# Linear attention on one core: the keys' products with values issued every fourth step instead of every second

## The chip, the cores and the metric

The kernel runs on one core of one Trainium2 chip. The metric is the device time of one execution in microseconds (us). Before the change three runs took 2346.34, 2346.76 and 2348.77 us, a median of 2346.76 us. Engines are named as the profile names them: PE is TensorE (matmuls), PEld its loads of weights, DVE is VectorE, ACT is ScalarE, POOL is GpSimd, SP is SyncE, from whose queue most DMAs are issued.

## What is computed

A decoder layer on x of 2 sequences x 2048 tokens x 512, in float32: linear attention, cross attention to 154 context tokens, and a mixture of eight experts with two shared units. The change touches the linear attention alone (16 heads of 32, 128 features a head):

```python
qkv = x @ w_qkv                       # x is layernormed
q_proj = _elu1(jnp.einsum('bhnd,hdf->bhnf', q, proj_matrix))
k_proj = _elu1(jnp.einsum('bhnd,hdf->bhnf', k, proj_matrix))
kv = jnp.einsum('bhnf,bhnd->bhfd', k_proj, v)
attn = jnp.einsum('bhnf,bhfd->bhnd', q_proj, kv)
k_sum = k_proj.sum(axis=2)
z = 1.0 / (jnp.einsum('bhnf,bhf->bhn', q_proj, k_sum) + 1e-08)
out = (attn * z[..., None]).reshape(b, n, d) @ w_out + b_out
```

## The kernel before

**Tiling.** The 4096 tokens are 8 blocks of 512, four to a sequence. A block has four chunks of four heads (128 columns of the model), and a chunk has four tiles of 128 tokens. So the keys take 8 x 4 x 4 = 128 steps n, one for each (block, chunk, tile).

**The loop of the key steps (L1277 to L1304).** Step n does five things in program order:

1. `dense.fill` (L1279) issues some nine or ten matmuls from a list of projections waiting to be made: keys (`pk`), values (`pv`) and queries (`pq`), and near the end the context's keys and values (`xpk`, `xpv`). Each is a chain of 12 full 128x128 matmuls of 512 columns. `dense` also counts matmuls for things that are due later, such as reading a stored tile back (`dense.after`).
2. `key_features` (L393): four matmuls `pp` (L402) into a PSUM bank of the pool `sc` (four banks), then Relu and Exp on ACT (L364, L365) and a combination on DVE (L366) into `e_k`, 128x512, and an addition into `kacc` on POOL (L407). `e_k` is one of nine buffers of the tag `kp` (L102), which other tiles share.
3. (b, c, t) is appended to the list `todo` (L1297).
4. From n = 66 on, `query_step` (L1257) makes the features of one head of the queries of the sequence whose keys are done: one matmul `pqp` (L479), then the same ACT and DVE work into `e_q` (head 0, tag `kp`) or `eq` (heads 1 to 3, a pool of five buffers, L83).
5. On some steps, `sums_step` (L1265). It makes `key_values` (L410) for all of `todo` but the last two entries, the newest first, and, when the queries' step is the last head of a chunk (h == 3), the numerators (L485) and denominators (L507) of the chunk before.

**Column matmuls.** `key_values`, `numerators` and `denominators` use a stationary operand of 32 columns and write 32 partitions of PSUM, one head at a time: `pkv[h*32:(h+1)*32]`, `pn`, `pd`. The trace shows each of them as 128*32 and counts two instructions for each of the program's matmuls (1024 for the 512 of `pkv`). They go through a helper, all at line L230:

```python
def matmul(self, *args, **kw):
    ins = nc.tensor.matmul(*args, **kw)
    tc.keep_in_program_order(ins)
```

The rest of the order on each engine is set by the framework's scheduler, which also picks the buffer of each tile. A group of L230 matmuls with no other matmul between them is called a run here.

**The condition before** is `n % 2 and len(todo) > LAG` with LAG = 3: sums are made at every odd n from 3 on, two tiles' products at a time. On n with n % 4 == 1 (from 69 on) the numerators and denominators follow in the same call; on n with n % 4 == 3 the call has only the two tiles' products.

**After the 128 steps** six more (L1305) finish the sums of the second sequence; `summary` (L430) turns the products over for use by the queries. The queries of the second sequence follow with the attention's output projection (L1317 to L1356), then cross attention (L1360) and the experts (L1457).

Of the kernel before, what the change touches and what calls it, by code (L numbers as in the profile page):

```python
# [31 lines left out]
LAG = 3  # L32
# [5 lines left out]
def decoder_layer(  # L38
# [62 lines left out]
    def half(name, dtype=F32):  # L101
        return work.tile([P, 512], dtype, tag="kp", name=name, bufs=9)  # L102
# [8 lines left out]
    def load_row(d, name):  # L111
        row = rowp.tile([P, D], F32, tag="row", name=name)
        nc.sync.dma_start(out=row, in_=d.to_broadcast([P, D]))
        return row
# [11 lines left out]
    def split_weight(raw, name, busy=False):  # L126

        hi = eight([P, NC, D], FR, f"{name}_hi")
        lo = eight([P, NC, D], FR, f"{name}_lo")
        for k in range(NC):  # L130
            if isinstance(raw, list):
                part = raw[k]
            else:
                part = load_tile(raw, 0, k, name)
            if busy:
                nc.gpsimd.tensor_scalar(hi[:, k], part, 1.0, None, ALU.mult)
            else:
                nc.scalar.copy(hi[:, k], part)
            low(lo[:, k], part, hi[:, k], nc.gpsimd if busy or k % 2 else nc.vector)
        return hi, lo  # L140
# [94 lines left out]
    def fl(k, f):  # L235
        return int((k + 1) * f + 1e-6) - int(k * f + 1e-6)
# [156 lines left out]
    def key_features(b, c, t):  # L393
        if (b % bpb, c, t) == (0, 0, 0):
            bt = b // bpb
            kaccs.append(eight([P, H * FEAT], F32, f"kacc{bt}"))
            nc.gpsimd.memset(kaccs[bt], 0.0)
        rows = slice(t * P, (t + 1) * P)
        pp = sc.tile([P, 4, FEAT], F32, tag="sc", name=f"pp{b}_{c}_{t}")
        for h in range(4):  # L400
            head = slice((4 * c + h) * FEAT, (4 * c + h + 1) * FEAT)
            nc.tensor.matmul(  # L402
                pp[:, h], lhsT=stks[b, c][:, h, rows], rhs=pst[:, head], start=True, stop=True
            )
        kp = features(pp.rearrange("p h f -> p (h f)"), f"k{b}_{c}_{t}")
        acc = kaccs[b // bpb][:, c * 512 : (c + 1) * 512]
        nc.gpsimd.tensor_tensor(acc, acc, kp, ALU.add)  # L407
        kps[b, c, t] = kp
# [63 lines left out]
    def load_queries(b, c):  # L472
        qsts[b, c] = eight([3 * HD, 4, TB], FR, f"qst{b}_{c}")
        stack(qsts[b, c], qd[b][c])
# [69 lines left out]
    def load_numerators(b):  # L544
        nums[b] = eight([P, NC, TB], F32, f"num{b}")
        nc.gpsimd.dma_start(out=nums[b], in_=numd[b])

    def load_reciprocals(b, c):
        two = pair_of(f"zr{b}_{c}").bitcast(F32)
        for h in range(4):  # L550
            nc.sync.dma_start(
                out=two[h * HD : (h + 1) * HD],
                in_=zds[b][h : h + 1, c : c + 2].to_broadcast([HD, 2, TB]),
            )
        for i in range(2):
            zrs[b, c + i] = two[:, i]
# [41 lines left out]
    def context_load():  # L598
        craw = eight([P, NC, nkeys], F32, "craw")
        nc.sync.dma_start(out=craw, in_=chunked(ctx_t))  # L600
        for i in range(2):
            ct.append(eight([P, NC, nkeys], FR, f"ct{i}"))
        nc.scalar.copy(ct[0], craw)
        low(ct[1], craw, ct[0], nc.gpsimd)

    def context_key(c, w):
        pk = bank(f"xpk{c}")[:, :nkeys]
        yield from project(pk, w, c * P, ct)
        kf = half(f"kf{c}")[:, :nkeys]
        nc.vector.tensor_scalar(kf, pk, bk_sb[:, c : c + 1], scale, ALU.add, ALU.mult)  # L610
        hl = pair_of(f"xkhl{c}", nkeys)
        nc.scalar.copy(hl[:, 0], kf)
        low(hl[:, 1], kf, hl[:, 0])
        store_pair(ckd[c], hl)

    def context_value(bt, first, w, row):
        n = min(P, keys - first)
        at = bt * keys + first
        pv = bank(f"xpv{bt}_{first}")
        yield from product(  # L620
            pv[:n, :],
            [
                (
                    (ct[0][:, k, at : at + n], ct[1][:, k, at : at + n]),
                    (w[0][:, k, :], w[1][:, k, :]),
                )
                for k in range(NC)
            ],
        )
        v = half(f"v{bt}_{first}")  # L630
        nc.vector.tensor_tensor(v[:n], pv[:n, :], row[:n], ALU.add)
        nc.sync.dma_start(out=vd[bt][first : first + n], in_=v[:n])
# [619 lines left out]
    todo = []  # L1252
# [4 lines left out]
    def query_step(m):  # L1257

        at, h = divmod(m, 4)
        if at < bpb * NC:  # L1260
            if h == 0 and at + 1 < bpb * NC:
                load_queries(*chunks[at + 1])
            query_features(*chunks[at], h)

    def sums_step(m):  # L1265


        columns.batch()
        ready = len(todo) if m >= (nblk - bpb) * per - shift else len(todo) - LAG + 1
        for i in reversed(range(ready)):  # L1270
            key_values(*todo.pop(i))
        at, h = divmod(m, 4)
        if m >= 0 and at and h == 3:
            numerators(*chunks[at - 1])
            denominators(*chunks[at - 1])

    for n in range(nblk * per):  # L1277
        b, c, t = n // per, n // NT % NC, n % NT
        dense.fill(58 if n == 0 else fl(n, 9.25) if n < 32 else fl(n, 9.5))  # L1279
        if (b, c, t) == (nblk - 1, 0, 0):  # L1280
            context_load()
        if (b, c, t) == (nblk - 1, 1, 0):
            xwk = split_weight(wk_t, "xwk")
            dense.add(*(context_key(i, xwk) for i in range(NC)))
        if (b, c, t) == (nblk - 1, 2, 0):
            xwv = split_weight(wv_t, "xwv")
            bvr = half("bvr")
            nc.sync.dma_start(out=bvr, in_=bv.to_broadcast([P, D]))
            for bt in range(batches):
                dense.add(*(context_value(bt, at, xwv, bvr) for at in range(0, keys, P)))  # L1290
        if (b, c, t) == (nblk - 1, 3, 0):
            load_numerators(0)
            load_reciprocals(0, 0)
            bout = load_row(b_out, "bout")
        dense.until(stks, (b, c))
        key_features(b, c, t)
        todo.append((b, c, t))  # L1297
        m = n - bpb * per - shift
        if m == -4:
            load_queries(0, 0)  # L1300
        if m >= 0:
            query_step(m)
        if n % 2 and len(todo) > LAG:
            sums_step(m)  # L1304
    for m in range((nblk - bpb) * per - shift, (nblk - bpb) * per + NT):  # L1305
        dense.fill(5)
# [150 lines left out]
    for n, (group, u) in enumerate(todo3):  # L1457
# [18 lines left out]
        for s, part in enumerate(parts):  # L1476
# [19 lines left out]
            if ahead[0]:  # L1496
                (ln, tr), (ln2, tr2) = ahead
                todo = (ln, [], tr[:2], tr[2:] + ln2, [], tr2[:2], tr2[2:])
# [89 lines left out]
```

## Time and profile before

| what | value |
|---|---|
| median of the three runs | 2346.76 us |
| the profiled execution, its own time | 2340.21 us |
| its span, first to last instruction | 2338.5 us |
| mean granted clock of PE in it | 0.984 |
| PE busy in the span | 2241.0 us, 96% |
| DVE, POOL, ACT busy | 72%, 52%, 47% |
| L230 `pkv`, instructions | 1024, from 44.5 to 475.7 us |
| L230 `pn` and `pd`, instructions | 512, from 263.0 to 641.2 us |

How to read it: busy times are sums over one execution, and a matmul's duration overlaps that of the next, so the distance from start to start tells what a matmul costs and the duration doesn't. In a timeline, x16 means sixteen instructions merged into one row; the bracket at the end gives idle time of the engine before the row and what ended it. PEclk is the granted share of PE's full clock. A row of a windows view has the stretch, its length, then the busy time of each engine with its count of instructions, the granted clock, the share of the DMA engines' time and GB/s.

### The profile page before, as it was taken

The numbers are of one execution on the slowest core, as the hardware profiler recorded it, in microseconds if no ns is written. First come the engines' busy times: TensorE is split into PE (matmuls) and PEld (weight loads), VectorE is DVE, ScalarE is ACT, GpSimd is POOL, SyncE is SP. The second block draws the span as 40 slices with busy tenths as digits, with TensorE's granted clock in tenths as the row PEclk, the third lists the DMA queues.
The fourth block names the chain that finished last, engine by engine and source line by source line (L and its number), as shares of the span: only waits on it lengthen the run. The fifth ranks groups of instructions, "written<-read, shape, count | busy, mean of one in ns | idle before, by whom it ended". The sixth has DMA issues, their size and how long they took to land.

```text
span 2338.5 us, 35133 instructions
## 1 busy us (share of the span) xinstructions
PE 2241.0 (96%) x11978; PEld 1733.3 (74%) x11978; DVE 1680.3 (72%) x2777; ACT 1104.9 (47%) x2598; POOL 1223.2 (52%) x1086
## 2 busy tenths in 40 slices
PE   7999999899989999999999999999999999999999
PEld 5888777655577777766777777888778887788887
DVE  6554555668577776877877786777887778977777
ACT  4555776756566766775343333222333222432221
POOL 5545433547475554553655554544564455754543
PEclk9999999999999999999999999999999999999999
DMA  6555778899965665565665646555447556575553
GB/s 210 180 171 174 208 210 228 248 255 266 258 201 159 173 175 155 172 199 203 243 240 221 223 175 258 209 222 207 158 180 275 207 207 236 193 276 202 211 189 131
DMA packets 194896, 485.63 MB, mean 208 GB/s; under 512 B 26970, under 2 KB 46810, under 8 KB 174782
## 3 DMA queue, kind: packets, MB, share of 16 engines
q1 hardware_dynamic: 192990, 477.30, 61.5%
q0 software_dynamic: 1728, 6.09, 0.9%
q8 instruction: 95, 1.56, 0.3%
q14 instruction: 83, 0.68, 0.1%
HBM read 345.01 MB, written 138.31 MB: 207 GB/s over the span
## 4 chain that ended last, share of the span: by engine, by line
PE 48%; DVE 9%; DMA 5%; POOL 4%; issue 3%; ACT 2%; SPq 0%; ACTq 0%; DVEq 0%; POOLq 0%
PE pg L1053 25%; PE pf L1166 10%; PE po_x L148 3%; PE pf L148 2%; PE xpq L148 2%; PE pc L745 2%; PE xpt L725 1%; PE psc L693 1%; DMA rgu<-in_w_up 1%; DVE u L1073 1%; DVE xo L118 1%; POOL hp L118 1%; DVE wq L118 1%; DVE u L1085 1%; DMA xsx<-x 1%
## 5 line engine op out<-in xcount | busy, mean ns | idle before, releaser
L1053 PE MATMUL pg<-xo,wq 128*128 128x512 f32 x3360 | 825.7, 393 | 7.2 <-ACT s L1064 3.5
L1053 PEld LDWEIGHTS pg<-xo,wq 128*128 128x128 f32 x3360 | 630.2, 189 | 149.3 <-ACT s L1064 7.1
L1187 DVE TENSOR_TENSOR sum<-sum,pf 128x512 f32<-128x512 f32 x376 | 250.5, 682 | 61.1 <-PE pf L1166 53.5
L407 POOL TENSOR_TENSOR kacc<-kacc,e_k 128x512 f32<-128x512 f32 x128 | 165.9, 1297 | 225.6 <-DVE e_k L366 203.6
L703 ACT ACTIVATE xe<-psc,nb 128x154 f32<-128x154 f32 x512 | 194.4, 403 | 63.0 <-DVE nb L700 47.4
L708 POOL TENSOR_TENSOR xe<-xe,sm 128x616 f32<-128x616 f32 x128 | 156.7, 1232 | 108.1 <-DVE sm L707 73.7
L1116 POOL TENSOR_TENSOR u<-u,gr 128x512 f32<-128x512 f32 x48 | 63.8, 1328 | 255.7 <-DVE u L1085 244.3
L1166 PE MATMUL pf<-ht,wdo 128*128 128x512 f32 x696 | 187.4, 393 | 1.0 <-DVE sum L1187 1.0
L366 DVE SCALAR_TENSOR_TENSOR e_k<-pp,e_k 128x512 f32<-128x512 f32 x128 | 87.4, 685 | 107.9 <-ACT e_k L365 101.8
L1166 PE MATMUL pf<-hb,wdo 128*128 128x512 f32 x522 | 148.2, 399 | 6.0 <-DVE sum L1187 5.9
L1166 PEld LDWEIGHTS pf<-ht,wdo 128*128 128x128 f32 x696 | 129.8, 188 | 30.7 <-DVE sum L1187 1.7
L1084 ACT ACTIVATE u<-u 128x512 f32<-128x512 f32 x80 | 50.6, 633 | 211.1 <-DVE u L1073 208.5
L148 PE MATMUL pf<-wd,hp 128*128 128x512 f32 x528 | 134.0, 400 | 6.2 <-DVE hp L118 3.0
L700 DVE TENSOR_REDUCE nb<-psc 128x2 f32<-128x308 f32 x256 | 111.9, 467 | 31.1 <-PE psc L693 30.9
L148 PEld LDWEIGHTS pf<-wd,hp 128*128 128x128 f32 x528 | 99.7, 190 | 33.1 <-DVE hp L118 3.9
L1166 PEld LDWEIGHTS pf<-hb,wdo 128*128 128x128 f32 x522 | 97.4, 189 | 30.4 <-DVE sum L1187 7.7
L1073 DVE TENSOR_TENSOR u<-u,pg 128x512 f32<-128x512 f32 x160 | 107.7, 679 | 10.5 <-PE pg L1053 9.7
L703 ACT ACTIVATION_READ_ACCUMULATOR xe<-psc,nb 128x1 f32 x512 | 111.6, 218 | 0.0
L364 ACT ACTIVATE e_k<-pp 128x512 f32<-128x512 f32 x128 | 76.8, 601 | 69.9 <-PE pp L402 64.4
L693 PEld LDWEIGHTS psc<-xkst,xst 96*128 96x128 f32 x512 | 76.1, 193 | 35.2 <-ACT xe L703 18.9
L693 PE MATMUL psc<-xkst,xst 96*128 96x154 f32 x512 | 90.3, 284 | 12.3 <-ACT xe L703 8.4
L402 PEld LDWEIGHTS pp<-pst,kst 96*128 96x128 f32 x512 | 75.8, 191 | 26.8 <-issue 9.9
(280 smaller groups left out, 5143.2 us busy)
## 6 DMA issues: line engine op xcount, KB each, us to landing
wq<-wqs SPq DMA_DIRECT2D x90, 1024.0 KB
wqs<-wq SPq DMA_DIRECT2D x30, 1024.0 KB
wdo<-wds SPq DMA_DIRECT2D x29, 1024.0 KB
kst<-kd SPq DMA_DIRECT2D x96, 256.0 KB
qst<-qd SPq DMA_DIRECT2D x96, 256.0 KB
xst<-xqd SPq DMA_DIRECT2D x96, 256.0 KB
wdo<-wds SPq DMA_DIRECT2D x29, 768.0 KB
kd<-khl SPq DMA_DIRECT2D x32, 512.0 KB
```

The costliest lines, as they stand in the source:

```text
L148: nc.tensor.matmul(dst, lhsT=a, rhs=b, start=n == 0, stop=n == len(todo) - 1)
L364: nc.scalar.activation(e, src, AF.Relu, scale=-1.0)
L366: nc.vector.scalar_tensor_tensor(e, src, 0.0, e, ALU.max, ALU.add)
L407: nc.gpsimd.tensor_tensor(acc, acc, kp, ALU.add)
L693: nc.tensor.matmul(psc[:, i], lhsT=xsts[b, c][:, h, t * P : (t + 1) * P], rhs=ksts[bt, c][:, h, :], start=True, stop=True,)
L700: nc.vector.tensor_reduce(nb[:, two], psc, AX.X, ALU.max, negate=True)
L703: nc.scalar.activation(e[:, h, :], psc[:, i], AF.Exp, bias=nb[:, h : h + 1], accum_out=sm[:, h : h + 1],)
L708: nc.gpsimd.tensor_tensor(e, e, sm.unsqueeze(2).to_broadcast([P, 4, keys]), ALU.mult)
L1053: nc.tensor.matmul(pb, lhsT=w[:, p, i, k, :], rhs=xop[:, q, k, :], start=first and m == 0, stop=m == len(todo) - 1, skip_group_check=True,)
L1073: nc.vector.tensor_tensor(dst, dst, pb, ALU.add)
L1166: nc.tensor.matmul(banks[i], lhsT=w[:, p, i * P : (i + 1) * P], rhs=t[q], start=new and m == 0, stop=m == len(TERMS) - 1, skip_group_check ...
L1187: nc.vector.tensor_tensor(dst, dst, banks[i], ALU.add)
```

## The change

One condition in the loop of the key steps:

```diff
         if m >= 0:
             query_step(m)
-        if n % 2 and len(todo) > LAG:
+        if n % 4 == 1 and len(todo) > LAG:
             sums_step(m)
```

`sums_step` is now called at n = 5, 9, ... 125, and each call makes the products of four tiles instead of two. The queries' step is m = n - 66, so that n % 4 == 1 is h == 3: every call that makes numerators and denominators is still made, at the same step, with four tiles' products ahead of them in place of two. What is not called any more is `sums_step` at n = 3, 7, ... 127. At the time of a call `todo` holds six tiles in place of four, so six `e_k` buffers of the nine are held rather than four. The last entries, which the call at n = 127 took before, are taken by the first call after the loop (m = 63).

Every matmul, activation and DMA of the program is there as before, in the same number; the scheduler, which sees another list, also places others of them differently, on every engine.

## The prediction

> **What bounds the kernel now.** I read the page first, then the busy times by stretch, then who makes PE wait, and last the order of PE's instructions in time around the L230 runs. The page:
>
> ```profile
> PE 2241.0 (96%) x11978; PEld 1733.3 (74%) x11978; DVE 1680.3 (72%) x2777; ACT 1104.9 (47%) x2598; POOL 1223.2 (52%) x1086
> PE   7999999899989999999999999999999999999999
> ```
>
> PE is busy 96% of the span. A mean says little, so the stretch that the change touches (keys, 44 to 480 us) is read by itself. Two rows of the windows view:
>
> ```profile
> 100.00:160.00 60.00, 60.00 (x434) 48.55 (x433) 34.36 (x55) 34.33 (x60) 30.18 (x32) 1.00 0.60 186
> 432.00:480.00 48.00, 41.16 (x303) 27.92 (x303) 30.03 (x45) 31.05 (x60) 23.05 (x18) 0.93 1.01 295
> ```
>
> From 100 to 432 us PE is busy nearly all the time (97% or more in each row) at full clock, the other engines between 34 and 75%, DMA 58 to 76%. From 432 to 480 us PE is at 86% and the DMA engines are full; DMA stays at 0.92 to 0.93 until 645 us. PE's waits from 100 to 432 us are these, in all 1.6 us of 332:
>
> ```profile
> PE pqp L479 <- DVE eq L366: 0.8, 1, 0.8
> PE ptks L459 <- DVE ks L455: 0.5, 1, 0.5
> PE pd L230 <- DVE xl_a L118: 0.3, 1, 0.3
> ```
>
> So up to 432 us PE's own stream is the time: what leaves it, leaves the total. After 432 us this holds less surely (waits on DVE and DMA of some 20 us until 647).
>
> **What a run costs.** No matmul goes away. What changes is how often PE passes from full matmuls to 32-column ones and back. PE's timeline without a run after `pp`, then with one (the two `pp` rows are the same work):
>
> ```profile
> 120.93 0.56 PE L402 MATMUL pp<-pst,kst 96*128 96x128 f32 x4
> 121.32 0.44 PE L148 MATMUL pv<-wv_hi,xl_a 128*128 128x512 f32 x1
> 121.61 0.39 PE L148 MATMUL pv<-wv_lo,xh_a 128*128 128x512 f32 x1
> ...
> 123.46 0.56 PE L402 MATMUL pp<-pst,kst 96*128 96x128 f32 x4
> 123.95 0.65 PE L230 MATMUL pkv<-e_k,va 128*32 128x128 f32 x16
> 124.52 0.50 PE L148 MATMUL pv<-wv_hi,xl_a 128*128 128x512 f32 x1
> 124.86 0.39 PE L148 MATMUL pv<-wv_lo,xh_a 128*128 128x512 f32 x1
> ```
>
> From `pp` to the second `pv`: 121.61 - 120.93 = 0.68 us without, 124.86 - 123.46 = 1.40 us with. A run of two tiles costs 0.72 us. Between two dense matmuls, which else start 0.23 us apart, it costs 0.05 more (0.32 into it, 0.57, 0.34 to the second matmul behind it, less 2 x 0.23: 0.77). Now the same 16 `pkv` inside a longer run, with and without them:
>
> ```profile
> 277.93 0.64 PE L230 MATMUL pkv<-e_k,va 128*32 128x128 f32 x16
> ...
> 280.22 0.67 PE L402 MATMUL pp<-pst,kst 96*128 96x128 f32 x4
> ```
>
> ```profile
> 307.73 0.63 PE L230 MATMUL pn<-eq,kv 128*32 128x512 f32 x3
> ...
> 309.58 0.66 PE L402 MATMUL pp<-pst,kst 96*128 96x128 f32 x4
> ```
>
> 280.22 - 277.93 = 2.29 us against 309.58 - 307.73 = 1.85 us: inside a run the two tiles cost 0.44 us. A run that is merged into another therefore saves 0.72 - 0.44 = 0.28 to 0.77 - 0.44 = 0.33 us; I take 0.31.
>
> **How many runs.** The order of PE's instructions in the two built programs has 96 runs of L230 before and 54 after. The plan removes 31 or 32; ten more go because the scheduler used to put a `pq`, `pp` or `pt` between parts of a call (five splits into 3 and 5 matmuls, some between `pn` and `pd`). Up to the last `pd` at 432 us it is 69 against 32, 37 fewer: 37 x 0.31 = **11.5 us** (10.4 to 12.2), all in the stretch where PE is the time. Behind it 5 fewer, up to 1.6 us, where PE also waits for others: 0.7.
>
> **The start.** Here the order changes by more than the runs:
>
> ```profile
> 43.50 1.09 PE L402 MATMUL pp<-pst,kst 96*128 96x128 f32 x4 [4.46 <-DMA kst<-kd]
> 44.52 1.08 PE L230 MATMUL pkv<-e_k,va 128*32 128x128 f32 x16
> 45.53 0.80 PE L148 MATMUL pq<-xh_a,wq_hi 128*128 128x512 f32 x1
> ...
> 50.16 0.56 PE L402 MATMUL pp<-pst,kst 96*128 96x128 f32 x4
> ```
>
> PE waits 4.46 us for the second chunk's keys. In the changed program the twelve `pq` and one transpose stand ahead of that `pp`. They take 12 x 0.23 + 0.35 = 3.1 us at full clock, and their operands are there (the last `wq_lo` is written by 27 us, the transposed tile normalised near 31 us). They fill the wait: **3.1 us** less; 0 if a PSUM bank or the next keys are late instead (the third chunk's reads were issued from 45.0 to 46.3 us; landing some 5 us later, as the second's did, they are there near 51 us, and would be used near 52).
>
> The wait costs a second time. The stretch 39.1 to 42.5 has no matmul, and 42.5 to 49.4 is at a granted clock of 0.51 and 0.50, where the `pq` start 0.43 apart in place of 0.23: about 3.4 us lost. With 1.4 us of waiting left, a 3.4 us stretch would be 0.6 busy. The nearest rows go both ways: 711.5 to 715.0, busy 0.61 (2.12 of 3.50), and 459.0 to 462.4, 0.62, are followed by a clock of 0.50; 1117.7 to 1121.1, 0.60, by 1.00. So I take half, **1.7 us**, ends 0 and 3.4.
>
> The Trainium skill, "TensorE: Matmul & The Clock Gate", section "Why this matters for your kernels", asks only that idle gaps between bursts stay under about 3 us. By it the shorter wait would give back the whole 3.4 us and the sum would be 1.7 us lower. The row at 459.0 differs: PE's waits there are single ones of 1.1 us and less, and the clock was halved.
>
> **What is delayed.** Step by step:
>
> - ACT's Relu of `eq` for head 3 waits for the end of the run that frees one of the five `eq` buffers (13.8 us in ten waits from 260 to 432 us). The run is longer by 0.44 us, so each of some 15 such waits is too. Behind it on ACT stand the next `e_k` and the copies of projections. ACT is busy 43 of 60 us there (340 to 400), so 0.44 in some 14 us is covered by its slack: 0. Without that cover it would be 15 x 0.44 = 6.6 us.
> - Six `e_k` are held of nine buffers. In the built order the reader that frees a buffer for an `e_k` stands a median of 61 matmuls before the `pp` that feeds the new one (98 before the change), and behind it in one case: the second `e_k` of the very last chunk, whose Relu waits for a run 9 matmuls later. There `kf`, `num` and `bvr` share the nine. DVE's `kf` and `num` wait for that same run. Before, PE waited 1.1 and 0.3 us at this place (461 to 463); I add **1.5 us**, 0 to 4.
> - The DMAs keep their number; SP's queue has the same issues in a slightly other order. PE reaches each earlier, so reads of stored keys have the same time after their store: 0.
> - Behind 480 us the order on PE, DVE and ACT differs in small ways up to the experts. Its price isn't in the trace. PE's waits from 432 to 647 us sum to some 20 us, and a halved clock window costs 1.7 us: I bound it by a third of those waits, 6 us either way, and take 0.
>
> The Trainium skill speaks against the change in "Perfetto Trace Analysis", section "Optimization Strategy": a gap that repeats on the engine that should be saturated can mean too few buffers for the next tile. The trace of before has no such gap between 100 and 432 us (1.6 us of waits). The two more held buffers could make one; that is the slower rival below.
>
> **The sum.** -11.5 - 0.7 - 3.1 - 1.7 + 1.5 = -15.5 us. The profiled execution took 2340.2 us, 6.5 below the median of the runs; it would become 2324.7, and the median 2346.8 - 15.5 = **2331.3 us**. Ends: -12.2 - 1.6 - 3.1 - 3.4 - 6 = -26 (2320.5), and -10.4 + 4 + 6 = 0 (2346.8).
>
> **Rivals.**
>
> *Given back behind 432 us.* The DMA engines are full from 432 to 480 us and over 0.9 busy to 645, and one chain there ends in DMAs (DVE waits 5.9 us for the denominators' round trip at 446.6, then PE 3.6). If that stretch ends by what the DMA engines moved and not by when it began, some or all of the gain turns into waiting: -5 to -11 if a part, 2346 if all. Against it: its DMAs are issued as PE goes on, so they start earlier too, and DMA is only 0.75 busy just before.
>
> *Slower: buffers.* Where the tags run short, Relu waits on ACT, DVE's work behind it waits, the four `sc` banks stay full and PE stops at the next `pp`, once in each of 31 calls. From 0.5 us a call the gain is gone; at 0.9 us it is 28 us and the time 2359. For it: a third of `kp` more is held for longer, and ACT already waits 13.8 us on runs. Against it: 61 matmuls are some 14 us of lead.
>
> *No change in the runs.* The scheduler could split the longer calls again. The built order has one split of 33, so this is nearly out.
>
> **How the numbers follow.** The forecast's own cases (-11 to -26): 0.62. Partly given back: 0.15. All given back: 0.14. Slower, by buffers or by the reordering behind: 0.09. About 0.2%, 4.7 us, is what a measurement of this kernel can tell from no change. Faster: 0.62 + 0.15 = 0.77; within it 0.14; slower 0.09. The range runs from the far end of the forecast, 2321, to 2345, which leaves out the slower case and part of the unchanged one.
>
> **What would show it.** Right: 54 groups of L230 in PE's timeline, four tiles' `pkv` lasting about 1.0 us from start to the next matmul, 0.44 more in front of `pn`; the wait for `kst` near 40 us down from 4.46 to about 1.4; `pn` of the last chunk before 432 us some 15 us earlier, and everything behind it by as much. Wrong: PE waits on DVE `e_k` or `eq` that repeat between 100 and 432 us, or a stretch from 432 to 650 us that is longer by what was won before.

## The result

The changed kernel takes 2357.28 us (median of six runs, 2353.03 to 2363.8) against 2346.82 (six runs, 2344.46 to 2349.11): a ratio of 1.0047, 95% interval 1.0036 to 1.0058. It is slower by about 10 us where 15.5 us less were forecast. Its profiled execution took 2354.09 us, with a span of 2352.3. The two profiled executions lie 13.8 us apart in their spans and the medians 10.5: the one before is 6.5 us below its median, the one after 3.2. The page after, the same two rows as in the prediction:

```profile
PE 2239.8 (95%) x11978; PEld 1740.2 (74%) x11978; DVE 1678.5 (71%) x2777; ACT 1100.5 (47%) x2598; POOL 1219.0 (52%) x1086
PE   7999999888989999999999999999999999999999
```

PE's busy time is smaller by 1.2 us and its span is longer by 13.8: PE waits more. The windows view after:

```profile
100.00:160.00 60.00, 57.76 (x429) 47.63 (x429) 34.22 (x55) 33.27 (x60) 30.71 (x33) 0.97 0.62 189
432.00:480.00 48.00, 41.59 (x341) 30.78 (x339) 32.87 (x48) 34.09 (x66) 23.85 (x19) 0.92 0.98 283
```

In the first stretch PE had no idle time and full clock before; now 2.2 us are idle and the clock is 0.97. PE's waits from 100 to 432 us, 1.6 us in three waits before, are 13.3 us now, most of them here:

```profile
PE pp L402 <- DMA kst<-kd: 6.2, 3, 3.0
PE pq L148 <- DVE xl_a L118: 2.4, 1, 2.4
PE pp L402 <- DVE e_k L366: 2.1, 2, 1.6
PE pqp L479 <- DVE eq L366: 1.9, 2, 1.3
```

**Where the time goes.** The table gives the start of the same matmul in both profiled executions (a quarter of `pp` is the matmul behind which three quarters of them are still to come):

| matmul | before, us | after, us | after - before |
|---|---|---|---|
| a quarter of `pp` | 132.7 | 126.3 | -6.4 |
| half of `pp` | 229.3 | 225.1 | -4.1 |
| first `pn` | 263.1 | 264.2 | +1.1 |
| nine tenths of `pp` | 418.8 | 424.5 | +5.7 |
| last `ptkv` (end of the keys) | 477.2 | 482.0 | +4.8 |
| first `po_a` | 505.9 | 508.7 | +2.9 |
| first `psc` (cross attention) | 637.7 | 651.3 | +13.6 |
| last matmul | 2334.3 | 2348.1 | +13.8 |

There are three parts: a gain at the start, a loss of 12.1 us from 126 to 425, and a loss of 10.7 us between the first `po_a` and the first `psc`, a stretch in which the change edits nothing. Behind it the difference goes up and down (+20.5 at the first `po_x` of the cross attention, +12.3 at the first `pg` of the experts) and ends where it was.

Each column is a single execution. The run e10, further down, shows how far that can be trusted: its lists on TensorE, VectorE, ScalarE and GpSimd are those of the changed kernel up to 477 us, and it is 4.8 us ahead of it at half of `pp` and 2.7 at the last `ptkv`. e9 and the kernel before, nearly the same list up to 475 us, differ by 1.5 us at most at the same places. So a difference of 3 us between two single executions, here and in what follows, can be chance.

**The saving per run is there.** PE's timeline at the start and around a merged run:

```profile
42.87 0.39 PE L148 MATMUL pq<-xl_a,wq_hi 128*128 128x512 f32 x1
43.10 0.60 PE L259 MATMUL pt_a<-ident,xsa 128*128 128x128 f32 x4
44.10 1.08 PE L402 MATMUL pp<-pst,kst 96*128 96x128 f32 x8 [0.40 <-DMA kst<-kd]
...
118.41 0.40 PE L148 MATMUL pv<-wv_hi,xl_a 128*128 128x512 f32 x1
118.74 1.08 PE L230 MATMUL pkv<-e_k,va 128*32 128x128 f32 x32
119.75 0.50 PE L148 MATMUL pv<-wv_lo,xh_a 128*128 128x512 f32 x1
120.09 0.40 PE L148 MATMUL pv<-wv_hi,xh_a 128*128 128x512 f32 x1
```

The wait of 4.46 us for `kst` is 0.40 us now. A run of four tiles costs 120.09 - 118.41 - 2 x 0.23 = 1.22 us between dense matmuls, two runs of two tiles 2 x 0.77 = 1.54: each merge saves 0.32 us (0.31 taken). In the changed kernel too, inside a call with numerators the step from `pkv` to the next matmul behind `pd` is 2.73 us with 32 `pkv`; it was 2.29 with 16. There are 54 runs, as worked out.

**What the keys lose.** From a quarter to nine tenths of `pp` the kernel before takes 286.1 us with 49 runs; after, 298.2 us with 23. By the runs alone it would be 286.1 - 26 x 0.33 = 277.5, so 20.7 us are lost anew. The waits make 13.3 - 1.6 = 11.7 of them. Behind the longer waits the granted clock is 0.5 for a window of 3.41 us: at 151.0, 236.4, 321.7 and twice at 413.9, and not once in this stretch before. Five windows at half the clock cost 5 x 1.7 = 8.5 us. Together 20.2 of the 20.7. It is no chance: e10 and e11, which have the same lists up to there, take 297.8 and 297.1 us for this stretch.

The first of the three waits for `kst` shows how it comes about. PE, then SP's queue:

```profile
146.36 0.64 PE L402 MATMUL pp<-pst,kst 96*128 96x128 f32 x4
149.24 1.19 PE L402 MATMUL pp<-pst,kst 96*128 96x128 f32 x9 [2.24 <-DMA kst<-kd]
```

```profile
138.78 0.38 SPq L300 DMA_DIRECT2D kd<-khl  x1
143.80 1.27 SPq L294 DMA_DIRECT2D kst<-kd  x3
```

The keys are stored at 138.78, read back from 143.80 and there at 149.2, over 10 us after the store. In the kernel before 24 `pq` stood between the last `pk` of this chunk and its first `pp`, 13.5 us apart (143.54 and 157.07). Now twelve stand there (138.01 to 140.57, the last `pk` at 136.94), and twelve more behind that `pp`, from 150.26 on. So PE comes to the `pp` 10.1 us after the last `pk`, 2.24 us before its keys are there.

**The queries.** The stretch from 508 to 651 us, before and after, with the waits of PE that grew:

```profile
508.00:651.00 143.00, 128.99 (x653) 82.14 (x651) 101.15 (x160) 80.77 (x157) 79.67 (x74) 0.97 0.93 258
...
PE pqp L479 <- DVE e_q L366: 4.3, 2, 2.2
PE pqp L479 <- DMA qst<-qd: 1.5, 2, 0.9
```

```profile
508.00:651.00 143.00, 128.73 (x619) 79.89 (x612) 98.83 (x147) 78.35 (x145) 74.62 (x69) 0.96 0.92 253
...
PE pqp L479 <- DVE e_q L366: 7.2, 8, 2.4
PE pqp L479 <- DMA qst<-qd: 2.7, 1, 2.7
```

PE starts 619 instructions where it started 653, DVE 147 for 160. No engine is much busier or idler; everything is a little late, in eight short waits for `e_q` where there were two.

### The profile page after: what moved, and what is told of

Read it like the earlier page. It is cut to its first block, busy times and chain, and to the rows that moved or that the text cites. A ratio compares the mean times of both kernels' runs of the same rounds, so it can differ in the third digit from the quotient of the medians.

```text
span 2352.3 us, 35108 instructions
## 1 busy us (share of the span) xinstructions
PE 2239.8 (95%) x11978; PEld 1740.2 (74%) x11978; DVE 1678.5 (71%) x2777; ACT 1100.5 (47%) x2598; POOL 1219.0 (52%) x1086
## 4 chain that ended last, share of the span: by engine, by line
PE 51%; DMA 9%; DVE 8%; POOL 5%; issue 4%; ACT 2%; SPq 1%; POOLq 0%; DVEq 0%; ACTq 0%
PE pg L1053 25%; PE pf L1166 10%; PE po_x L148 3%; PE xpq L148 3%; PE pf L148 2%; PE pc L745 2%; PE xpt L725 2%; PE psc L693 2%; DMA zr<-zd 1%; DMA xr_x<-x 1%; DMA x<-xr_a 1%; POOL num L563 1%; POOL hp L118 1%; DMA xsx<-x 1%; DMA wq<-wqs 1%
```

## The experiments

Each ratio is against runs of the kernel before that were made in turn with it on the same chip. e1 to e4, e5 to e8, e9 to e12 and e13 to e15 are four such groups; across groups the ratios are compared.

### The change in one half of the loop

```diff
-        if n % 2 and len(todo) > LAG:
+        if (n % 4 == 1 if n < bpb * per else n % 2) and len(todo) > LAG:   # e1
+        if (n % 2 if n < bpb * per else n % 4 == 1) and len(todo) > LAG:   # e2
```

> The sums are made every fourth step only for n below 64 (keys of the first sequence, no queries' steps beside them), every second step after it, as before. Its order on PE differs from that of before only up to the first 15% of PE's instructions and in a stretch of the experts. Theory O (order): a merged run saves 0.31 us as predicted, and what was lost is the scheduler's new order, which puts pp ahead of the dense matmuls that covered the keys' round trip through DMA. It expects the start's gain of some 6 us, 20 fewer runs (6 us) and waits for kst near 147, 198 and 233 us that take about that back: 2340 to 2348. Theory B (buffers): six held e_k are too many, and only where e_q and num share the nine buffers, which is from n = 66 on. It expects the plain gain here, 2335 or less, and no wait between 100 and 230 us.

> The reverse: every second step for n below 64, every fourth after it. Its order on PE differs from that of before from the queries' first steps to the end of the queries, and nowhere behind. Theory O: 22 fewer runs (7 us), against waits that the new order makes between 260 and 650 us; where the order of the second sequence's queries is that of before (it nearly is), the loss of 10 us between 508 and 650 us doesn't come: 2338 to 2347. Theory B: the loss sits here, 2353 or more, with waits of DVE and ACT on runs that free e_k buffers.

| | ratio | 95% interval | half of `pp` | last `ptkv` | first `po_a` | first `psc` |
|---|---|---|---|---|---|---|
| e1, first sequence (76 runs) | 1.0002 | 0.9987 to 1.0016 | -6.4 | -4.8 | -2.9 | +0.1 |
| e2, second sequence (75 runs) | 1.0031 | 1.0015 to 1.0048 | 0.0 | +3.0 | +0.3 | +3.4 |

The last four columns are us against the kernel before, from the profiled executions. Theory O had e1 right, with its waits: `pp` waits for `kst` 2.27, 0.86 and 2.16 us (ending at 147.1, 196.5 and 232.9), with a halved window behind the two longer ones (148.3 and 233.6). Its lead of 6.4 us at half of `pp` is 2.3 by 245. Theory B's plain gain did not come. e2 has the calls with numerators, and is slower without any gain at the start; its 2351.58 us lie between the ranges of the two theories.

e1 also shows where a lead ends. From 274 us to the experts its list on TensorE is that of the kernel before, and by the last `ptkv` it is 4.8 us ahead again; at the last `ptks`, 7.3 us later, it is level (479.73 and 479.72). On VectorE only the places of the `at` differ between 276 and 500 us: one of them now stands ahead of `ks`, which PE's `ptks` needs, and it waits, through ScalarE and GpSimd, for the reciprocals read back from DRAM (`zr`). e1, then the kernel before:

```profile
475.35 2.48 POOL L563 TENSOR_TENSOR num<-num,zr 128x512 f32<-128x512 f32 x2 [3.41 <-DMA zr<-zd]
477.29 1.08 DVE L118 TENSOR_TENSOR at<-num,at 128x512 fp32r<-128x512 f32 x1 [3.88 <-ACT at L564]
478.30 0.68 DVE L455 COPY ks<-pks 128x512 f32<-128x512 f32 x1
479.03 1.11 PE L459 MATMUL ptks<-ident,ks 128*128 128x128 f32 x4 [4.92 <-DVE ks L455]
```

```profile
478.59 0.69 DVE L455 COPY ks<-pks 128x512 f32<-128x512 f32 x1 [0.39 <-PE pks L447]
479.34 0.66 PE L459 MATMUL ptks<-ident,ks 128*128 128x128 f32 x4 [0.43 <-DVE ks L455]
480.03 2.80 DVE L118 TENSOR_TENSOR at<-num,at 128x512 fp32r<-128x512 f32 x2 [0.74 <-ACT at L564]
```

The reciprocals themselves are earlier in e1 (`num` at 475.35 against 478.08). It is the order on VectorE, which the scheduler chose anew, that hands the lead back here.

### The order on TensorE held

e3 and e4 hold the two kinds of feature matmuls in program order, with the old and the changed condition:

```diff
-            nc.tensor.matmul(
+            tc.keep_in_program_order(nc.tensor.matmul(
                 pp[:, h], lhsT=stks[b, c][:, h, rows], rhs=pst[:, head], start=True, stop=True
-            )
+            ))
...
-        nc.tensor.matmul(pp, lhsT=pst[:, head], rhs=qsts[b, c][:, h, :], start=True, stop=True)
+        tc.keep_in_program_order(nc.tensor.matmul(pp, lhsT=pst[:, head], rhs=qsts[b, c][:, h, :], start=True, stop=True))
```

> The kernel before with pp and pqp (the features' matmuls of keys and queries) pinned behind whatever PE instruction was traced before them, so that the scheduler can't move them forward. 83 runs of L230. Theory O: near 2347, or less where a hoisted pp made PE wait (4.46 us at 39 us go): 2338 to 2350. Theory B says nothing of it. It is the base for the next one.

> The changed kernel with the same pins: 51 runs, 32 fewer than with the pins and the old condition, and up to the end of the queries nearly the same order of everything else. Theory O: faster than the pinned kernel with the old condition by 32 x 0.31 = 10 us (7 to 12). Theory B: as slow against it as the changed kernel was against before, 8 to 14 us slower, with PE's waits on DVE e_k and eq repeating. A third theory, R (round trip): PE's pace in the key steps is set by the keys' way through DMA, about 12 us from pk to pp, so whatever PE saves turns into waits for kst: within 3 us of it.

e3: 2341.33 us, ratio 0.9992 (0.9978 to 1.0006), 83 runs. e4: 2345.21 us, 1.0009 (0.9994 to 1.0023), 51 runs. With the order held the waits for `kst` are gone, so these came from the order that the scheduler chose and not from the longer runs. None of the three theories of e4 came true: it is neither faster by 7 to 12 us nor slower by 8 to 14, and 3.9 us behind e3 without a wait for `kst`. The gain of the keys is now in plain sight, and so is its end. e4 against e3: -4.1 us at a quarter of `pp`, -5.0 at the first `pn`, -7.0 at nine tenths of `pv` (390.7 and 397.7), -3.0 at the last `ptkv`, +0.2 at the first `po_a` (507.2 and 507.0), +0.2 at the first `psc`. PE's largest waits of e4 between 432 and 508 us:

```profile
PE pqp L479 <- DVE eq L366: 5.7, 2, 5.4
PE ptks L459 <- DVE ks L455: 3.6, 1, 3.6
```

e3 has 4.6 (the longest 4.1) and 0.9 there. The first is PE's share of VectorE's wait for the denominators' round trip (`z` from `dd`, 6.13 us in e4 and 6.38 in e3). The second is the case of e1: the order of `pp` and `pqp` is held on TensorE, but on VectorE `ks` stands behind `at` in e4 and ahead of it in e3. `num` starts at 478.4 in e4 and 482.0 in e3, `ks` at 481.3 and 481.5; the granted clock is halved for 6.8 us from 480.6 on. So the lead of 3.0 us at the last `ptkv` is spent on a new wait. What would be left of it with `ks` ahead of `at` was not tried.

From the first `po_a` to the first `psc` e3 and e4 have the same list on TensorE, and take 133.3 and 133.4 us. With that order the changed condition costs nothing there, where the changed kernel lost 10.7.

e5 and e6 put the numerators and denominators ahead of the products in a call (old and changed condition), so that `eq` comes free sooner. e7 adds to e6 that the context is split two steps after its load, and the reciprocals of the first three blocks are taken later; e12 is e7 with the old condition.

```diff
-        for i in reversed(range(ready)):
-            key_values(*todo.pop(i))
         at, h = divmod(m, 4)
         if m >= 0 and at and h == 3:
             numerators(*chunks[at - 1])
             denominators(*chunks[at - 1])
+        for i in reversed(range(ready)):
+            key_values(*todo.pop(i))
...
-        dense.after(26 if b < nblk - 1 else 24, stored)
+        dense.after(45 if b < bpb - 1 else 26 if b < nblk - 1 else 24, stored)
...
-            context_load()
+            craw = context_load()
+        if (b, c, t) == (nblk - 1, 0, 2):
+            context_split(craw)
```

> The pinned kernel with the old condition, and in sums_step the numerators and denominators put ahead of the keys' products, so that a run frees the eq buffers 0.44 us sooner. Theory A (ACT held): ACT's wait for the run's end delays its next work, DVE's behind it and the PSUM bank of the next pq; each 0.1 us of run ahead of pd costs. It expects ACT's wait on pd down from 15 us by some 5, and 0 to 3 us less in all than the pinned kernel without the exchange: 0.998 to 1.000 of before. Theory R (round trip of the keys) and theory D (DMA behind 432 us sets the pace) expect no change against it.

> The same exchange in the pinned kernel with the changed condition: the four tiles' products, 0.87 us, come behind pn and pd, so the longer run no longer delays eq. Theory A: the loss of the pinned changed kernel (PE's waits on pq's bank 7.5 us against 3.5) goes; it is faster than the pinned changed kernel by 4 to 8 us and faster than the same with the old condition by 3 to 9: 0.995 to 0.998 of before. Theory D: PE's waits up to 400 us shrink, but the time from 507 us on is the same: within 2 us of both. Theory R: waits for kst in place of the others, no gain.

> As the one before, and two waits between 400 and 450 us taken away: the context's split on ACT and POOL comes two steps after its load in place of at once (ACT waits 3 to 4 us for it), and the reciprocal of the first three blocks' denominators comes 45 counted matmuls after the denominators in place of 26 (DVE waits 6 us for it near 446, PE then 4 to 5). Theory L: these two fixed latencies are where the gain of the key steps is handed back, so with them gone it stays: 5 to 10 us faster than the one before, 0.991 to 0.995 of before. Theory D: what is won at 400 to 450 us is waited for again before 507 us: within 2 us.

> Control of e7: its three edits (order of pp and pqp held, numerators ahead of the products, context split and reciprocals later) with the old condition. If e7's 0.17% come from the fewer runs of 32-column matmuls, this is 4 us slower than e7, at 1.000 to 1.001 of the kernel before, as e5 was. If they come from the later context split and reciprocals, it is at 0.998 too, and fewer runs are worth nothing in the total.

| | condition | median, us | ratio | 95% interval | ACT `eq` waits for `pd`, 100 to 432 us |
|---|---|---|---|---|---|
| e5 | old | 2350.6 | 1.0013 | 1.0002 to 1.0023 | 9.1 |
| e6 | changed | 2348.25 | 1.0007 | 0.9993 to 1.0021 | 10.9 |
| e7 | changed | 2343.22 | 0.9983 | 0.9970 to 0.9996 | 8.6 |
| e12 | old | 2346.6 | 1.0002 | 0.9987 to 1.0016 | 10.5 |

The exchange makes ACT's wait shorter (it is 15.1 us in e3 and 19.3 in e4, 13.8 before the change and 23.0 after it), and nothing is won: e6 is level with e4, and e5 is 0.21% above e3. Both had been expected lower (0.998 to 1.000 and 0.995 to 0.998), so that wait wasn't what decides. e7 is the one version that beats the kernel before by more than its interval, by 0.04 to 0.30%. It is 5.0 us below e6, the low end of what was expected of its two further edits, but above its range of 0.991 to 0.995. It is as much below e12 as expected (0.0019, some 4.5 us), though the two intervals overlap. In the profiles it is 6.9 us ahead of e12 at the last `pp`, behind by 2.1 at the first `po_a`, and ahead by 2.8 at the end; where the last 4.9 come from isn't settled. Part of the loss between is known: in e6 and e7 an `at` stands ahead of `kvt` on VectorE, and PE's `ptkv` waits 4.0 and 3.9 us for it, 1.5 in e5 and e12. So all four of e1, e4, e6 and e7 meet the same `at` at the end of the keys.

### The held buffers alone

e8 makes no call longer, but leaves four tiles in the list instead of two, so that six `e_k` are held as in the changed kernel; e15 is e8 with the order held as in e3.

```diff
-        ready = len(todo) if m >= (nblk - bpb) * per - shift else len(todo) - LAG + 1
+        ready = len(todo) if m >= (nblk - bpb) * per - shift else len(todo) - LAG - 1
...
-        if n % 2 and len(todo) > LAG:
+        if n % 2 and len(todo) > LAG + 2:
```

> The kernel before, but sums_step leaves four tiles in todo in place of two (two calls later for each tile), with runs as often as before: six e_k are held at a call, as in the changed kernel, and no run is merged. 94 runs. Theory B (buffers): slower than before by 5 us or more. Theories A and O: holding them costs nothing by itself; the order on PE is another one again, so 0.998 to 1.004 of before, and ACT's wait on pd stays near 14 us.

> e8 (six e_k held, no products merged) with the order of pp and pqp held as in e3. If e8's 0.5% were the two more buffers, it stays: first po_a at 512 us or later, ratio 1.004 and more. If they were the order that the scheduler chose for e8, the kernel comes near e3: ratio 0.998 to 1.002, no wait of PE on e_k between 100 and 400 us.

e8: 2361.57 us, 1.0054 (1.0036 to 1.0073). e15: 2355.1 us, 1.0027 (1.0012 to 1.0041). Neither of the two cases expected of e15 came whole. There is no wait of PE for `e_k` between 100 and 400 us, and e15 is level with e3 or ahead to the last `pp` (-4.2 us). Then it loses: +1.7 at the last `ptkv`, +5.0 at the first `po_a`, +7.5 at the first `psc`. Its longest waits of PE from 432 to 512 us, and one of POOL:

```profile
PE pp L402 <- DVE e_k L366: 4.8, 1, 4.8
PE ptks L459 <- DVE ks L455: 2.8, 1, 2.8
PE pkv L230 <- DVE e_k L366: 2.7, 1, 2.7
```

```profile
481.48 1.27 POOL L563 TENSOR_TENSOR num<-num,zr 128x512 f32<-128x512 f32 x1 [8.40 <-DMA zr<-zd]
482.71 1.28 POOL L407 TENSOR_TENSOR kacc<-kacc,e_k 128x512 f32<-128x512 f32 x1
```

The first ends at 450.0, behind a wait of 7.07 us of VectorE for the denominators' round trip; e3 has that too (6.38, seen there as the 4.1 of `pqp` for `eq`). A wait for a buffer is in the trace as well: at 444.5 the Relu of an `e_k` waits 3.8 us for the store of a `num` (2.4 in e3), and e15 is still ahead at the last `pp`. What it loses comes behind that. On ScalarE the last `e_k` stands behind an `eq` that waits 2.2 us for its `pqp`; on GpSimd the last `kacc` stands behind the `num` above, on VectorE `ks` behind two `at` (+1.7 at the last `ptkv`, +6.1 at the last `ptks`). So the two more buffers cost nothing up to the last `pp`. Behind it e15 loses some 9 us, by waits of which the trace puts none down to a buffer; whether the scheduler put these lists together so because of the held buffers isn't shown. e8 has another order again, and is slower still.

### The order of the second sequence's queries

e9 and e10 hold every full matmul and every query matmul from L1317 to L1356 in program order, on the kernel before and on the changed one. e11 holds the query matmuls L479 alone (the second line of e4's diff) in the changed one.

```diff
-            nc.tensor.matmul(dst, lhsT=a, rhs=b, start=n == 0, stop=n == len(todo) - 1)
+            ins = nc.tensor.matmul(dst, lhsT=a, rhs=b, start=n == 0, stop=n == len(todo) - 1)
+            if inorder[0]:
+                tc.keep_in_program_order(ins)
```

> The kernel before, with every full matmul and every query matmul from L1317 to L1356 (queries of the second sequence, attention's output projection) held in program order on TensorE. Only the control for the next run: holding the order may cost or save some us by itself; both theories expect the time of the kernel before plus 0 to 15 us, and nothing changed up to 480 us.

> The changed kernel with the same part held: behind the last ptks its list on TensorE is now the same, instruction by instruction, as that of the control. Theory A (the 10 us that the changed kernel loses from 508 to 651 us are its other order there): the stretch from the first po_a to the first psc is as long in both (within 2 us), and the whole is 0 to 4 us above the control, which is what the changed kernel is late by at 508 us. Theory B (they come from what the keys leave behind, DMAs and buffers that are late): the stretch stays 8 to 11 us longer than the control's, and the whole 10 to 14 us.

> The changed kernel with the query matmuls L479 alone held in program order; the keys' order is left as the scheduler of the changed kernel has it, waits for kst included. Theory A: the first psc comes near 641 us in place of 651 and the time is within 0.2% of the kernel before. Theory B: first psc near 650 us, 0.4% above the kernel before.

| | ratio | 95% interval | first `po_a` | first `psc` | between |
|---|---|---|---|---|---|
| before | | | 505.9 | 637.7 | 131.8 |
| after | 1.0047 | 1.0036 to 1.0058 | 508.7 | 651.3 | 142.6 |
| e9, before held | 1.0046 | 1.0027 to 1.0064 | 512.7 | 648.5 | 135.8 |
| e10, after held | 1.0054 | 1.0032 to 1.0076 | 508.9 | 648.2 | 139.3 |
| e11, after, L479 held | 1.0023 | 1.0005 to 1.0040 | 509.4 | 646.1 | 136.7 |

e9 is the strongest run of the study. Its list on TensorE is that of the kernel before, instruction by instruction but for the order inside one group of eight `pn` at 263 us, up to the first query matmul of the second sequence near 475 us; nothing is added and nothing taken away; and it is slower by as much as the changed kernel. Its waits from 508 to 652 us are of another kind (its lines stand one to five further down than those of the kernel before):

```profile
PE pn L233 <- DVE xr_a L318: 5.8, 2, 3.6
PE pqp L482 <- DMA qst<-qd: 4.9, 1, 4.9
```

Of its 10.7 us at the first `psc`, 5.3 are there at the last `ptks`: in e9 too `ks` stands behind two `at` on VectorE, and PE waits 5.1 us for it. So an order of the same work from 475 us on is worth 10 us, as much as the whole loss. With the same order on TensorE from the last products to the end e9 and e10 reach the first `psc` together (648.5 and 648.2), and their ratios can't be told apart: no trace of the changed keys is left there, which speaks for theory A, as e3 and e4 do. e10 does not keep theory A's number of 2 us: the stretch is 3.5 us longer than in e9, because e10 enters it 3.9 us sooner and leaves it at the same time. e11, whose list on TensorE is that of the changed kernel up to 480 us, gets half of the loss back (5.2 us at the first `psc`; 641 was expected, 646.1 came). It has the order of e3 in about the first half of the stretch and that of the changed kernel behind it.

### What ends the last chunk

e13 and e14 are e3 and e4 with less to read. For ten chunks a third of the stored queries isn't read; the rows that meet the low part of the projection are set to zero, and that part of the features is left out.

```diff
-        stack(qsts[b, c], qd[b][c])
+        if b * NC + c in range(8, 18):
+            stack(qsts[b, c][: 2 * HD], qd[b][c], (0, 1))
+            nc.gpsimd.memset(qsts[b, c][2 * HD :].bitcast(F32), 0.0)
+        else:
+            stack(qsts[b, c], qd[b][c])
```

> e3 (old condition, order of pp and pqp held) with a third of the reads of the stored queries left out for ten chunks, those read from about 370 us on: the rows that meet the low part of the projection are set to zero on GpSimd instead, so that this part of the queries' features is missing. Some 2 MB less for the DMA engines between 400 and 510 us, which at the 285 GB/s of that stretch is an estimated 7 us of their time. Theory C (the stretch to the first po_a ends by the DMA engines): first po_a at 500 to 504 us in place of 507. Theory D (it ends by something else, PE's order or the chain over DVE): 506 to 508.

> The same on e4 (changed condition, same order held). Theory C: what the keys have won by 390 us (7 us there in e4 against e3) is no longer handed back: first po_a 4 to 7 us ahead of e13, at 494 to 499 us. Theory D: first po_a within 1.5 us of e13, as e4 was of e3, and the gain is gone there too.

e13: 2349.07 us, 1.0009 (0.9994 to 1.0025), first `po_a` at 506.8. e14: 2343.79 us, 0.9987 (0.9974 to 1.0000), first `po_a` at 501.0. From 432 to 480 us, e13 and then e14:

```profile
432.00:480.00 48.00, 39.81 (x322) 28.07 (x322) 33.67 (x47) 33.73 (x64) 30.53 (x23) 0.96 0.97 284
```

```profile
432.00:480.00 48.00, 35.80 (x285) 25.27 (x287) 28.53 (x44) 29.16 (x55) 29.67 (x22) 0.89 0.92 257
```

e14 is 7.2 us ahead of e13 at nine tenths of `pv`, 5.8 at the first `po_a` and 7.1 at the first `psc`, and 5.3 in the medians, where e4 was behind e3 by 3.9. Theory C was right on that difference (4 to 7 us) and wrong on both places: 506.8 in place of 500 to 504, 501.0 in place of 494 to 499. And the difference does not show that a lead was kept. At the last `ptkv` e14 is only 0.4 us ahead (474.9 and 475.4): its lead has gone at 460, where a buffer is short. VectorE's `kf` waits for the store of a `num` there, and PE for the `eq` behind it:

```profile
459.60 0.54 DVE L614 TENSOR_SCALAR kf<-xpk,bk_sb 128x308 f32<-128x308 f32 x1 [4.82 <-DMA numd<-num]
460.79 0.79 PE L483 MATMUL pqp<-qst,pst 96*128 96x512 f32 x1 [5.29 <-DVE eq L366]
```

Then e13 loses anew. GpSimd's last `kacc` stands behind a `num` that waits for `zr`, and `pks` waits for that `kacc`, which in e14 was made ahead of `num`, at 472.0:

```profile
475.61 2.50 POOL L567 TENSOR_TENSOR num<-num,zr 128x512 f32<-128x512 f32 x2 [4.43 <-DMA zr<-zd]
478.06 1.71 POOL L407 TENSOR_TENSOR kacc<-kacc,e_k 128x512 f32<-128x512 f32 x1
479.83 1.92 PE L447 MATMUL pks<-kacc,ones 128*32 128x512 f32 x2 [3.22 <-POOL kacc L407]
```

So this pair does not settle whether the DMA engines end the stretch: the share of the DMA engines in e13 (0.97) is that of e3 (0.96), the order on GpSimd and VectorE differs between the two, and the difference behind the last `ptkv` begins with a wait that comes from it.

## Why the prediction was wrong, step by step

- **A run and its number: right.** 0.31 us taken, 0.32 to 0.33 measured; 54 runs.
- **The start: right.** The wait went from 4.46 to 0.40 us, and the granted clock behind it no longer falls (1.00 from 40 to 100 us, 0.94 before). With the merges up to there 6.4 us were won by 126 us (8.5 in e10); 4.8 from the start and ten merges at 0.33 would be 8.1.
- **"The DMAs keep their number ... reads of stored keys have the same time after their store: 0": wrong, and the first step that failed.** Not PE's speed counts but how much work the new order puts between a chunk's keys and its first `pp`: 10.1 us where it was 13.5. In place of 0 it cost three waits, 6.2 us, and two halved windows, 3.4 us. Held in order (e4), they are gone.
- **ACT's Relu of `eq`, "covered by slack: 0": wrong in part.** The wait grew from 13.8 to 23.0 us (260 to 432 us). PE's waits for `e_k` and `eq` are 4.0 us, most of it near 412, with two halved windows, 3.4: about 7 us, near the price that the prediction gave without cover (6.6); that they come from ACT's wait is argued and not shown. The order moved too, and e6, in which ACT's wait is below that of the kernel before, is not faster. It is a part and not the cause.
- **Buffers, +1.5 (0 to 4): not seen in the changed kernel.** From 455 to 490 us PE waits there 1.5 us for an `e_k` in front of `pkv` and 0.9 for `ks`, no more than before (1.2 and 1.1 for `e_k`, 0.4 for `ks`). A wait for one of the nine buffers that reaches PE is in e14 (5.3 us at 460). The slower rival's form of it, a wait in each of 31 calls, did not occur.
- **"Its price isn't in the trace ... 6 us either way, and take 0", behind 480 us: wrong, and what stays in the total.** 10.7 us between the first `po_a` and the first `psc`. The bound was a third of the waits that were there before; e9 shows that a new order from 475 us on can cost 10.7 us by the first `psc`, more than half of them, and e4 that the changed condition costs nothing there in the order of e3. Waits that a good order avoids are not in the trace that has the good order, so the sum of those that it has doesn't bound them.
- **"What leaves it, leaves the total", and the rival "given back behind 432 us" (0.29 in the prediction's two cases): the rival was right on the number.** In e1 and in e4 against e3 the gain of the keys is gone by the first `psc` (-6.4 to +0.1, -7.0 to +0.2), and their times are level. Its reason, a stretch that ends by what the DMA engines moved, isn't shown. The last of the lead goes at the end of the keys, on `ks` or `kvt` behind an `at` that waits for a read from DRAM (3.6 to 4.9 us of PE in e1, e4, e6 and e7). Whether the forecast's 11.5 us would reach the total with VectorE's order held as well stays open. PE at 97% up to 432 us says that PE limits that stretch; it does not say that the next one starts when PE arrives.

So the price of a run was right, and the step that failed is the one that took the new order for free. In the keys the start and the merges won 15.0 us up to nine tenths of `pp` (6.4 and 8.6), and the new order lost 20.7; in the queries it lost 10.7, which stays. Open is how the order of e11's second half and the state at its start share the 8.4 us that it is still late by, and why e2 is slower by 0.31%: its longest wait is 6.5 us of a `pqp` at 452.4, behind VectorE's wait of 6.68 for the denominators, which the kernel before has shorter (3.6 and 5.88), but that is 3 us of the 7.

## What to carry to other kernels

An edit of some 10 us in a list of ten thousand instructions that a scheduler orders is priced with the order it brings: hold the order in both versions and measure that pair, before the edit itself is judged; and look at the lists of the engines that feed PE, since holding TensorE alone left `ks` free to change its place. A stretch in which PE is busy 97% gives its saving to the total only if the next stretch can begin sooner; look first at what PE needs there, and at what stands ahead of it on its engine and waits for a round trip over DRAM. And a wait can cost PE more than its length, by the halved clock behind it.

## What had not been expected of the hardware

The half clock can follow shorter waits than I had thought. In the changed kernel single waits of 2.24, 3.02 and 2.44 us in otherwise full stretches (147.0, 233.0, 319.1) were each followed by one window of 3.41 us at a granted clock of 0.5; one of 0.97 us at 197.9 was not. It does not always follow: in e11, whose list is the same there, a wait of 2.67 us ends at 322.8 (the 2.44 of the changed kernel), and no halved window comes behind it. The Trainium skill, "TensorE: Matmul & The Clock Gate", section "Why this matters for your kernels", asks that gaps stay under about 3 us. By these rows 2.24 us can be too long already. In the whole execution the windows at half the clock make 97.0 us after the change and 75.6 before, which is 10.7 us of full work. That is not the loss by another name: in e4 they make some 86 us and in e6 some 104, and neither is slower than the kernel before by more than its interval.
